# A macaron block on one core: the first stage's routing ahead of its shared expert, two bias adds on GpSimd, attention in two parts

## The chip, the cores and the metric

The kernel runs on 1 core of one Trainium2 chip, as one program. The metric is the device time of one execution in microseconds (us). Engines are named as the profile names them: PE (TensorE: matmul, and PEld its weight loads), DVE (VectorE), ACT (ScalarE), POOL (GpSimd), SP (SyncE, which here only issues DMA transfers). Each engine executes its own instruction stream in order and waits on semaphores for the others.

## The reference

The input is 8 batches of 1024 tokens of 256 values, fp32. A half-weighted feed-forward layer, linear attention and a second half-weighted feed-forward layer (same weights) follow each other, each on the layer norm of its input and added to it:

```python
x = x + 0.5 * ffn(layernorm(x))
x = x + attn(layernorm(x))
x = x + 0.5 * ffn(layernorm(x))

def ffn(xf):                      # xf: 8192 tokens x 256
    weights, idx = gate(xf)       # softmax over 16 experts; best 2 of the 4 groups, then the top 2
    combine = (one_hot(idx, 16) * weights[..., None]).sum(1)
    h1 = einsum('td,edi->tei', xf, We1) + be1      # 16 experts, inner size 128
    h3 = einsum('td,edi->tei', xf, We3) + be3
    yo = einsum('tei,eid->ted', silu(h1) * h3, We2) + be2
    y = einsum('te,ted->td', combine, yo)
    z = silu(xf @ ws1 + bs1) * (xf @ ws3 + bs3) @ ws2 + bs2   # shared expert, inner size 256
    return y + z

def attn(x):                      # per batch, 16 heads of 16 channels
    q, k, v = split(x @ w_qkv.T)
    q, k = relu(q), relu(k)
    z = 1 / (sum_n(k) . q + eps)
    context = v k^T               # per head, 16 x 16
    return (context q * z) @ w_proj.T + b_proj
```

Only the two chosen experts of a token are computed: tokens are scattered to rows of their experts in DRAM, processed there in blocks of rows, and the results are gathered.

## The kernel before, in words

All of it is one program with an automatic scheduler: the source issues work as Python generators that are advanced in turn (`run`), and the scheduler then orders each engine's instructions by their dependencies and that order of issue; only the expert blocks and the tail are in an order written out by hand. It has five stages, divided by barriers in the program's order.

- **Stage A** (rounds r = 0 to 8). Round r computes the layer norm of batch r (`normed`: L253 to L270) and its transposes (L283, L286), the routing of batch r-1 (`route`, L314) and the shared expert of batch r-2 (`shared_units`, L831). Of `route`, the gate's product pgT (L323), softmax, choice of groups and experts on DVE (L339 to L406), the rank of each token in its expert by a matmul (prk, L416), the row numbers rowi (L449) and weights cw (L433), and then on POOL the 16 scatters of rows (L467), four of them behind one iota (L456) and one tensor_scalar (L461). Of `shared_units`, per half batch: the bias bs2 (halved in `hb2`) is added to x on DVE (`add_bias`, L806), then p_s (L796), the activation and product hs_s (L800, L801), py_s (L815), and the addition to x (L819). Batch 7's routing is only begun here, and batch 7's shared expert is `late`: it is done from the end of blocks 0 on, with its bias behind the hidden layer. Finished x of batches 0 to 4 are stored to `xk` in DRAM.
- **Blocks 0** (`blocks`, L612). The scattered rows come back as xg, expert by expert: transposes pxg (L678), q (L699), hb (L705, L706), qy (L725), yo (L731), a scatter to ys (L736). The bias rows b2 (2.1 MB, loaded by SP at L236) lie in a pool of SBUF that is shared, by turns, with four of the six slots of xnT (`half`, L218; `shared_room["turn"]`); two slots are kept outside the pool. SP issues b2's loads first, then the first xg. All experts' weights are in `wall`, loaded once.
- **Stage C** (rounds r = 0 to 9). Round r advances together: `finish(r-2)`, which is the second norm and routing and then stores x to `xk` (L1056) and xnT to `xt`; `attention(r-1)`; `begin(r)`, which adds the experts' results y to x (`combine`, L856) and computes attention's norm and transposes; and the shared expert of batches 5 to 7. The x of batches 3 to 7 is loaded from `xk` (L110) at the start of the round before, into the slot of a batch that has been stored.
- In `attention` (L862), the bias of the projection is added to x first (L867, DVE, 128x2048). Then per tile of 128 tokens pk = k and q (L877), relu on ACT (L881, L882), and the products pgs (L885) summed over the batch; these are copied to gk (L892). From gk come dg (L896), pks (the sum of k, L901), pgt (L909); then on DVE q times the sum (L920), its sum per head (L923), its reciprocal, and q scaled (L929); pcx, pm (L946), the transposes of q (pt_q, L283), pp (L954), and the addition to x (L958). q lies in slots of `xn`, qk in slots of `k`, qT in slots of xnT.
- **Blocks 1** and the **tail**: the same blocks for the second layer, then the shared expert of batches 0 to 4, the gathered y and the output. They are not edited.

## Time and profile before

| what | value |
|---|---|
| time, median of 4 runs | 1370.07 us (1368.14 to 1380.86) |
| the profiled execution's own time | 1364.59 us |
| its span in the profile | 1362.9 us, mean granted PE clock 0.948 |
| stage A, to PE's last work | 0 to 235.7 us: PE busy 195.3, DVE 160.3, POOL 124.4 |
| PE waits for the first block's rows | 235.7 to 248.7 us |
| blocks 0 | 248.7 to 515 us: PE busy 226.6 |
| stage C | 515 to 990.4 us: PE busy 422.0, DVE 313.3, POOL 134.3 |
| blocks 1 | 990.4 to 1251 us: PE busy 228.6 |
| tail | 1251 to 1363 us: PE busy 104.0 |

The profile is of one execution. Busy times of different engines overlap, so they don't add up to the length of a stage. The ranks prk (L416) are computed once per batch and are used as marks: in stage A they start at 36.1, 66.5, 96.3, 124.4, 156.8, 187.9 and 216.9 us. In stage C the mark is attention's pks and pgt (L901, L909), at 571.5, 610.4, 658.6, 710.0, 763.7, 815.3, 859.9 and 927.0 us. Waits are given as the waiting engine, tile and line, then the one that it waited for. Matmuls of fp32 take two hardware instructions, so the counts are twice those in the code.

### The profile page before, as it was taken

The numbers are of one execution on the slowest core, as the hardware profiler recorded it, in microseconds if no ns is written. First come the engines' busy times: TensorE is split into PE (matmuls) and PEld (weight loads), VectorE is DVE, ScalarE is ACT, GpSimd is POOL, SyncE is SP. The second block draws the span as 40 slices with busy tenths as digits, with TensorE's granted clock in tenths as the row PEclk, the third lists the DMA queues.
The fourth block names the chain that finished last, engine by engine and source line by source line (L and its number), as shares of the span: only waits on it lengthen the run. The fifth ranks groups of instructions, "written<-read, shape, count | busy, mean of one in ns | idle before, by whom it ended". The sixth has DMA issues, their size and how long they took to land. (4 is left out here: it accounts for less than half of the span.)

```text
span 1362.9 us, 20671 instructions
## 1 busy us (share of the span) xinstructions
PE 1176.6 (86%) x5728; PEld 844.0 (62%) x5728; DVE 884.2 (65%) x2878; ACT 539.7 (40%) x1120; POOL 585.9 (43%) x719
## 2 busy tenths in 40 slices
PE   7899778687789987999878879899998888998997
PEld 3465444576678874566546546555576677886554
DVE  6786547575456667767748648627686545665687
ACT  6566422221225542554453544543422223553110
POOL 1566556376655651002252252350536665565010
PEclk9999889798999998999889889999998899999999
DMA  9334323466565534632452430110435565552996
GB/s 358 140 126 168 122 90 119 141 189 184 184 188 173 171 121 148 212 123 97 138 203 87 132 126 29 37 64 1 157 114 170 179 198 170 150 173 90 334 373 247
DMA packets 96102, 212.20 MB, mean 156 GB/s; under 512 B 17382, under 2 KB 45291, under 8 KB 92273
## 3 DMA queue, kind: packets, MB, share of 16 engines
q1 hardware_dynamic: 68288, 134.77, 31.4%
q0 software_dynamic: 27696, 76.07, 15.0%
q8 instruction: 49, 0.80, 0.3%
q14 instruction: 69, 0.56, 0.1%
HBM read 110.75 MB, written 102.64 MB: 157 GB/s over the span
## 5 line engine op out<-in xcount | busy, mean ns | idle before, releaser
L736 POOL DMA_INDIRECT ys_d<-yo,at x276 | 278.5, 1009 | 226.5 <-DVE rest L731 161.7
L699 PE MATMUL q<-xgT,wc 128*128 128x128 f32 (+1 forms) x1568 | 283.5, 330 | 60.3 <-ACT xgT L683 41.9
L467 POOL DMA_INDIRECT xs_d<-xn_f,rowi x256 | 265.2, 1036 | 110.7 <-issue 60.8
L699 PEld LDWEIGHTS q<-xgT,wc 128*128 128x128 f32 x1568 | 231.5, 196 | 88.7 <-ACT xgT L683 52.6
L683 ACT COPY xgT<-pxg 128x512 f32<-128x512 f32 x138 | 81.3, 590 | 283.3 <-PE pxg L678 132.0
L796 PE MATMUL p_s<-xnT_f,ws_sb 128*128 128x512 f32 x352 | 168.2, 618 | 0.9 <-ACT hs_s L800 0.8
L706 DVE SCALAR_TENSOR_TENSOR hb<-q,wc,hb 128x128 f32<-128x128 f32 (+1 forms) x196 | 73.5, 400 | 132.6 <-PE q L699 42.6
L725 PE MATMUL qy<-wall,hb 128*128 x552 | 146.2, 388 | 6.8 <-DVE rest L731 6.6
L731 DVE CUSTOM_DVE_ANT_0 yo<-qy,b2c,at 128x256 f32<-128x256 f32 x276 | 122.8, 482 | 43.3 <-PE qy L725 7.3
L815 PE MATMUL py_s<-ws_sb,hs_s 128*128 128x256 f32 x512 | 128.6, 393 | 17.0 <-DVE hs_s L801 9.1
L815 PEld LDWEIGHTS py_s<-ws_sb,hs_s 128*128 128x128 f32 x512 | 96.4, 195 | 52.4 <-issue 16.8
L877 PE MATMUL pk<-wqk_sb,xnT_a 128*128 128x512 f32 x256 | 125.4, 607 | 0.5 <-ACT q L882 0.3
L461 POOL TENSOR_SCALAR xn_f<-cw 128x4 f32<-128x4 f32 x64 | 17.1, 274 | 248.0 <-DVE cw L433 245.1
L725 PEld LDWEIGHTS qy<-wall,hb 128*128 128x128 f32 x552 | 103.0, 196 | 21.5 <-issue 7.4
L800 ACT ACTIVATE hs_s<-p_s,bc 128x512 f32<-128x512 f32 x64 | 43.8, 687 | 182.0 <-PE p_s L796 124.4
L796 PEld LDWEIGHTS p_s<-xnT_f,ws_sb 128*128 128x128 f32 x352 | 68.1, 199 | 66.9 <-issue 62.2
L705 ACT ACTIVATE hb<-q,wc 128x128 f32<-128x128 f32 (+1 forms) x196 | 75.4, 421 | 69.9 <-PE q L699 37.2
L678 PE MATMUL pxg<-ident,xg 128*128 128x128 f32 x552 | 84.3, 277 | 12.9 <-DMA xg<-xs_d 12.9
L678 PEld LDWEIGHTS pxg<-ident,xg 128*128 128x128 f32 x552 | 69.8, 143 | 27.5 <-DMA xg<-xs_d 13.3
L801 DVE SCALAR_TENSOR_TENSOR hs_s<-p_s,bc,hs_s 128x512 f32<-128x512 f32 x64 | 47.7, 746 | 58.1 <-PE p_s L796 42.1
L885 PE MATMUL pgs<-xn_a,k 128*128 128x257 f32 x256 | 72.5, 400 | 8.2 <-issue 3.7
L796 PE MATMUL p_s<-xnTr,ws_sb 128*128 128x512 f32 x160 | 70.4, 593 | 0.3 <-PEq L786 0.3
(302 smaller groups left out, 1735.7 us busy)
## 6 DMA issues: line engine op xcount, KB each, us to landing
xg<-xs_d SPq DMA_DIRECT2D x80, 264.0 KB
y<-ys_d SPq DMA_DIRECT2D x64, 256.0 KB
y<-ys_d SPq DMA_DIRECT2D x32, 512.0 KB
xg<-xs_d SPq DMA_DIRECT2D x116, 132.0 KB
xk<-x SPq DMA_DIRECT2D x8, 1024.0 KB
x<-xk SPq DMA_DIRECT2D x8, 1024.0 KB
wall<-in_wexp_dram SPq DMA_DIRECT2D x4, 1540.0 KB
x<-in_x_dram SPq DMA_DIRECT2D x6, 1024.0 KB
```

The costliest lines, as they stand in the source:

```text
L467: nc.gpsimd.indirect_dma_start(out=v[:, :], out_offset=bass.IndirectOffsetOnAxis(ap=rowi[:, j, k : k + 1], axis=0), in_=xn[:, t, :], in_of ...
L678: nc.tensor.transpose(pt[:, c, s * P : (s + 1) * P], xg[i][:, s, c * P : (c + 1) * P], ident[:],)
L683: nc.scalar.copy(xgT[i][:], pt[:])
L699: nc.tensor.matmul(pt_[:, cs], w[:, s, o + c * P : o + (c + 1) * P], t[:, c, cs], start=(c == 0), stop=(c == NC - 1),)
L705: nc.scalar.activation(h[:, cs], p1[:, cs], AF.Silu, bias=w[:, s, W2 - 2 : W2 - 1])
L706: nc.vector.scalar_tensor_tensor(h[:, cs], p3[:, cs], w[:, s, W2 - 1 : W2], h[:, cs], ALU.add, ALU.mult)
L725: nc.tensor.matmul(py[:, s : s + 1, :], h[:, s * P : (s + 1) * P], w2s[s % len(w2s)], start=True, stop=True,)
L731: nc.vector.tensor_tensor_reduce(out=yo[:, s, :], in0=py[:, s, :], in1=b2c[s % len(w2s)][:, 0, :], scale=a[:, s, 1:2], scalar=0.0, op0=ALU ...
L736: nc.gpsimd.indirect_dma_start(out=ys_views[i * NR + s][:, :], out_offset=bass.IndirectOffsetOnAxis(ap=a[:, s, 0:1].bitcast(I32), axis=0), ...
L796: nc.tensor.matmul(pt[:], w[:, c, s * P : (s + 1) * P], xnT[:, c, :], start=(c == 0), stop=(c == NC - 1),)
L815: nc.tensor.matmul(py[:, t - t0, :], hs[s][:, t * P : (t + 1) * P], ws2_sb[:, s, :], start=(s == 0), stop=(s == NS - 1),)
L877: nc.tensor.matmul(pk.rearrange("p k d -> p (k d)"), tile_of(axnT, c, j), wqk_sb[:, c, :], start=(c == 0), stop=(c == NC - 1),)
```

## The change

Three edits.

First, in stage A `routed(b)` is the norm and the routing of the same batch, in the same round, and is advanced five steps for every two of the shared expert of batch r-2 (`weave`). Second, `hb2` is no longer added in stage A but in `begin(b)` of stage C, ahead of the y adds, and the projection's bias in `attention_q`; both are done by GpSimd, two adds of 128x1024 each per batch. The shared expert of the second layer keeps its bias add on DVE. Third, attention is split: `attention_k(b)` (k, q, pgs, gk) runs at the end of round b+1, `attention_q(b)` (the rest) in round b+2, beside `begin(b+2)` and `finish(b-1)`; stage C has 11 rounds instead of 10. q, qk and qT lie in space lent from `wall`, the part of experts 5 to 15, which is loaded again at the end of round 9. pcx moves from a PSUM buffer of tag p3 to one of tag y. The store of x to `xk` is issued at the start of `finish`, the loads of x at the end of a round.

```diff
@@ -141,10 +141,22 @@
     wv_sb = wp.tile([P, NC, D], F32, name="wv_sb")
     wproj_sb = wp.tile([P, NC, D], F32, name="wproj_sb")
 
+    HALF = TPB * D
+    E_KEPT = E - -(-8 * HALF // WROW)
+    def lent(i, name):
+        o = E_KEPT * WROW + i * HALF
+        return wall.rearrange("p e w -> p (e w)")[:, o : o + HALF]
+    def load_experts(lo):
+        for g in range(4):
+            es = slice(lo + g * (E - lo) // 4, lo + (g + 1) * (E - lo) // 4)
+            nc.sync.dma_start(out=wall[:, es, :], in_=wexp[:, es, :])
     def load_late_weights():
-        for g in range(4):
-            es = slice(g * E // 4, (g + 1) * E // 4)
-            nc.sync.dma_start(out=wall[:, es, :], in_=wexp[:, es, :])
+        load_experts(0)
         nc.sync.dma_start(out=wqk_sb[:], in_=w_qkT.rearrange("(c p) f -> p c f", p=P))
         nc.sync.dma_start(out=wv_sb[:], in_=w_v.rearrange("(c p) f -> p c f", p=P))
         nc.sync.dma_start(out=wproj_sb[:], in_=w_projT.rearrange("(c p) f -> p c f", p=P))
@@ -274,9 +286,9 @@
                 if t == HT - 1:
                     yield
 
-    def transposed(xns, name, res):
+    def transposed(xns, name, res, places=None):
         for nb, xn in enumerate(xns):
-            xnT = half("xnT", [P, NC, TB], f"xnT_{name}_{nb}")
+            xnT = places[nb] if places else half("xnT", [P, NC, TB], f"xnT_{name}_{nb}")
             for c in range(NC):
                 pt = ps_m.tile([P, TPB, P], F32, tag="m", name=f"pt_{name}_{nb}_{c}")
                 for t in range(TPB):
@@ -802,9 +814,9 @@
             h[:], p3[:], bc[:, NS + s : NS + s + 1], h[:], ALU.add, ALU.mult
         )
 
-    def add_bias(xh):
-        nc.vector.tensor_tensor(
-            xh, xh, hb2[:].unsqueeze(1).to_broadcast([P, HT, D]), ALU.add
+    def add_bias(xh, bias=hb2, engine=nc.vector):
+        engine.tensor_tensor(
+            xh, xh, bias[:].unsqueeze(1).to_broadcast([P, HT, D]), ALU.add
         )
 
     def outputs(xh, hs, name):
@@ -828,14 +840,14 @@
     def half_of(xt, nb):
         return xt[:, nb * HT : (nb + 1) * HT, :]
 
-    def shared_units(xt, xnT, name, late_bias=False):
+    def shared_units(xt, xnT, name, bias=True, late=False):
         for nb in range(NB):
             xh = half_of(xt, nb)
-            if not late_bias:
+            if bias:
                 add_bias(xh)
             hs = []
             for s in range(NS):
-                if late_bias and nb == 0:
+                if late and nb == 0:
                     hs.append(spare(f"hs_{name}_{nb}_{s}"))
                 else:
                     hs.append(
@@ -843,8 +855,6 @@
                     )
                 hidden(xnT[nb], s, hs[s], f"{name}_{nb}")
                 yield
-            if late_bias:
-                add_bias(xh)
             yield from outputs(xh, hs, f"{name}_{nb}")
 
     def combine(which, b, xt):
@@ -859,19 +869,19 @@
             yield
 
 
-    def attention(b, xt, axn, axnT):
-        kh, qh = [], []
+    def attention_k(b, axn, axnT):
+        kh = []
+        qh = [
+            lent(b % 2 * NB + nb, "q").rearrange("p (j d) -> p j d", d=D) for nb in range(NB)
+        ]
         pgs = [
             ps_h.tile([P, D + 1], F32, tag="p3", name=f"pgs_{b}_{c}") for c in range(NC)
         ]
-        nc.vector.tensor_tensor(
-            xt[:], xt[:], bpj[:].unsqueeze(1).to_broadcast([P, NT, D]), ALU.add
-        )
         for j in range(NT):
             nb, t = divmod(j, HT)
             if t == 0:
                 kh.append(half("k", [P, HT, D], f"k_{b}_{nb}"))
-                qh.append(half("xn", [P, HT, D], f"q_{b}_{nb}"))
             pk = ps_h.tile([P, 2, D], F32, tag="p1", name=f"pk_{b}_{j}")
             for c in range(NC):
                 nc.tensor.matmul(
@@ -890,6 +900,14 @@
         gk = big.tile([P, NC, D + 1], F32, tag="wc", name=f"gk_{b}", bufs=3)
         for c in range(NC):
             nc.scalar.copy(gk[:, c, :], pgs[c][:])
+        products[b] = (gk, qh)
+        yield
+    def attention_q(b, xt):
+        gk, qh = products.pop(b)
+        for nb in range(NB):
+            add_bias(half_of(xt, nb), bpj, nc.gpsimd)
 
         dg = mid.tile([P, NC, P], F32, tag="hb", name=f"dg_{b}", bufs=3)
         for c in range(NC):
@@ -916,9 +934,9 @@
         qT = []
         for nb in range(NB):
             den = rp.tile([P, HT, H], F32, tag="den", name=f"den_{b}_{nb}", bufs=1)
-            qk = half("k", [P, HT, D], f"qk_{b}_{nb}")
+            qk = lent(2 * NB + nb, "qk").rearrange("p (j d) -> p j d", d=D)
             nc.vector.tensor_tensor(
-                qk[:], qh[nb][:], ksb[:].unsqueeze(1).to_broadcast([P, HT, D]), ALU.mult
+                qk, qh[nb], ksb[:].unsqueeze(1).to_broadcast([P, HT, D]), ALU.mult
             )
             nc.vector.tensor_reduce(
                 den[:], qk.rearrange("p j (h d) -> p j h d", d=HD), axis=AX.X, op=ALU.add
@@ -933,7 +951,7 @@
 
         cm = mid.tile([P, NC, P], F32, tag="hb", name=f"cm_{b}", bufs=3)
         for c2 in range(NC):
-            pcx = ps_h.tile([P, P], F32, tag="p3", name=f"pcx_{b}_{c2}")
+            pcx = ps_y.tile([P, P], F32, tag="y", name=f"pcx_{b}_{c2}")
             for c in range(NC):
                 nc.tensor.matmul(
                     pcx[:], wv_sb[:, c, c2 * P : (c2 + 1) * P],
@@ -946,7 +964,10 @@
             nc.tensor.matmul(pm[:], cm[:, c2, :], wproj_sb[:, c2, :], start=True, stop=True)
             nc.scalar.copy(mm[:, c2, :], pm[:])
         yield
-        yield from transposed(qh, f"q{b}", qT)
+        places = [
+            lent(3 * NB + nb, "qT").rearrange("p (c n) -> p c n", c=NC) for nb in range(NB)
+        ]
+        yield from transposed(qh, f"q{b}", qT, places)
         for j in range(0, NT, 2):
             pp = ps_y.tile([P, 2, D], F32, tag="y", name=f"pp_{b}_{j}")
             for t in range(2):
@@ -972,6 +993,19 @@
                 if next(g, StopIteration) is StopIteration:
                     live.remove(g)
 
+    def weave(many, few):
+        run(many and groups(many, 5), few and groups(few, 2))
+    def groups(gen, n):
+        live = True
+        while live:
+            for _ in range(n):
+                live = live and next(gen, StopIteration) is not StopIteration
+            if live:
+                yield
     xns, xnTs = {}, {}
 
     def normed(which, b):
@@ -984,27 +1018,35 @@
 
     LATE = 3
     base = new_base(0)
+    begun = {}
+    def routed(b):
+        yield from normed(0, b)
+        if b == B - 1:
+            begun["maps"] = first_map(base, 0)
+        routing = route(base, 0, b, xns.pop(b), xnTs[b], b == B - 1)
+        if b == B - 1:
+            begun["routing"] = routing
+            routing = part(routing, 2)
+        yield from routing
     for r in range(B + 1):
         if r == 1:
             load_late_weights()
         if 2 <= r + 1 < B:
             xs[r + 1] = load_x(r + 1, x_v[r + 1])
         s = r - 2
-        routing = None
-        if r >= 1:
-            routing = route(base, 0, r - 1, xns.pop(r - 1), xnTs[r - 1], r == B)
-        if r == B:
-            maps, done, fill = first_map(base, 0)
-            steps = behind(routing, base, 0, maps, done, fill)
-        if r == B - 1:
-            run(routing)
-        run(
-            normed(0, r) if r < B else None,
-            routing if r < B else part(routing, 2),
-            shared_units(xs[s], xnTs.pop(s), f"s0_{s}") if s >= 0 else None,
+        weave(
+            routed(r) if r < B else None,
+            shared_units(xs[s], xnTs.pop(s), f"s0_{s}", False) if s >= 0 else None,
         )
         if 0 <= s < B - LATE:
             nc.sync.dma_start(out=xk_d[s][:], in_=xs.pop(s)[:])
+    maps, done, fill = begun["maps"]
+    steps = behind(begun["routing"], base, 0, maps, done, fill)
     tc.no_sync_barrier()
 
     def park(b, j):
@@ -1033,7 +1075,7 @@
         moves += [partial(fetch, b, j) for j in range(NT)]
 
     s = B - 1
-    late = shared_units(xs[s], xnTs.pop(s), f"s0_{s}", True)
+    late = shared_units(xs[s], xnTs.pop(s), f"s0_{s}", False, True)
     blocks(maps, 0, steps, by_block(moves), partial(steps_of, late, NS))
     for b in range(B - LATE, B - 1):
         xs.pop(b)
@@ -1042,18 +1084,23 @@
 
     room("rows1")
     base = new_base(1)
-    axns, last = {}, []
+    axns, products, last = {}, {}, []
 
     def begin(b):
+        for nb in range(NB):
+            add_bias(half_of(xs[b], nb), hb2, nc.gpsimd)
         yield from combine(0, b, xs[b])
         axns[b] = ([], [])
         yield from layernorm(xs[b], f"a{b}", axns[b][0], D + 1)
         yield from transposed(axns[b][0], f"a{b}", axns[b][1])
 
     def finish(b):
+        if b < B - LATE:
+            nc.sync.dma_start(out=xk_d[b][:], in_=xs[b][:])
         yield from normed(1, b)
         if b < B - LATE:
-            nc.sync.dma_start(out=xk_d[b][:], in_=xs.pop(b)[:])
+            xs.pop(b)
             for nb in range(NB):
                 nc.sync.dma_start(out=xt_d[b][nb], in_=xnTs[b][nb][:])
         if b == B - 1:
@@ -1064,21 +1111,25 @@
             routing = part(routing, 2)
         yield from routing
 
-    for r in range(B + 2):
-        if LATE <= r + 1 < B - 1:
-            xs[r + 1] = load_x(r + 1, xk_d[r + 1])
-        s = r - 3
+    for r in range(B + 3):
+        s = r - 4
         run(
             late if r == 0 else None,
-            finish(r - 2) if r >= 2 else None,
-            attention(r - 1, xs[r - 1], *axns.pop(r - 1)) if 1 <= r <= B else None,
+            finish(r - 3) if r >= 3 else None,
+            attention_q(r - 2, xs[r - 2]) if 2 <= r <= B + 1 else None,
             begin(r) if r < B else None,
             shared_units(xs[s], xnTs.pop(s), f"s1_{s}") if s >= B - LATE else None,
         )
+        if 1 <= r <= B:
+            run(attention_k(r - 1, *axns.pop(r - 1)))
         if r == 0:
             nc.sync.dma_start(out=xk_d[B - 1][:], in_=xs.pop(B - 1)[:])
-        if r == B - 2:
-            xs[B - 1] = load_x(B - 1, xk_d[B - 1])
+        if LATE <= r + 1 < B:
+            xs[r + 1] = load_x(r + 1, xk_d[r + 1])
+        if r == B + 1:
+            load_experts(E_KEPT)
     s = B - 1
     run(shared_units(xs[s], xnTs.pop(s), f"s1_{s}"))
     tc.no_sync_barrier()
```

## What I predict

> **What bounds the kernel now.** I read the page's head first, then the busy time by windows cut at the rank matmuls (prk, L416, one per batch), then the waits, then the groups. The profiled execution is 1364.59 us (span 1362.9); the median of the runs shown is 1370.07, 5.5 us more. I work against the first and add 5.5 at the end.
>
> Page, engines: busy us (share of span).
>
> ```profile
> span 1362.9 us, 20671 instructions
> PE 1176.6 (86%) x5728; PEld 844.0 (62%) x5728; DVE 884.2 (65%) x2878; ACT 539.7 (40%) x1120; POOL 585.9 (43%) x719
> ```
>
> TensorE (PE) is the busiest engine, but 86% is a mean. By stage: 0 to 235.7 us the first norm, routing and shared expert (stage A); 248.7 to 515 the expert blocks (blocks 0); to 990.4 combine, attention, second norm and routing (stage C); to 1251 blocks 1; then the tail. Only A and C are edited. Windows, one line per round, of A and then of C (columns: length, then busy us and count of PE, PEld, DVE, ACT, POOL; granted PE clock; DMA share; GB/s):
>
> ```profile
> 36.00:66.00 30.00, 24.56 (x117) 14.69 (x118) 21.86 (x87) 18.39 (x27) 17.57 (x24) 0.99 0.41 144
> 66.00:96.00 30.00, 28.45 (x123) 17.30 (x123) 26.84 (x83) 17.09 (x29) 20.95 (x24) 0.90 0.39 138
> 96.00:124.00 28.00, 25.93 (x121) 15.00 (x120) 21.79 (x75) 15.69 (x24) 18.57 (x27) 0.99 0.44 158
> 236.00:249.00 13.00, 0.34 (x2) 0.34 (x3) 1.76 (x6) 0.00 (x0) 5.94 (x10) 0.63 0.61 222
> ```
>
> ```profile
> 610.00:658.00 48.00, 42.11 (x218) 27.73 (x210) 31.91 (x101) 22.41 (x50) 17.60 (x26) 0.94 0.47 158
> 658.00:710.00 52.00, 42.10 (x206) 27.48 (x203) 34.56 (x104) 25.76 (x58) 17.89 (x27) 0.93 0.45 151
> 710.00:763.00 53.00, 45.01 (x197) 30.44 (x199) 34.80 (x103) 25.14 (x55) 17.29 (x25) 0.85 0.40 133
> 860.00:927.00 67.00, 62.32 (x265) 40.08 (x264) 34.20 (x87) 28.84 (x59) 21.90 (x31) 0.97 0.11 41
> ```
>
> A round of A lasts 30 us. Its matmuls at full clock (p_s 128x512 at 0.43 us, py_s 128x256 at 0.215, transposes 0.11) add up to 24.8. A round of C lasts about 50 for 38.2 of such work. No engine is full: a round is one long dependency through DVE, ACT and PE in turn, and PE, busy part of the time at a clock of 0.85 to 0.94, pays twice. The last two rounds of C differ: shared-expert work fills them (62 of 67 busy), so a shorter chain is worth nothing there.
>
> The waits say which steps end late (us in total, times, longest):
>
> ```profile
> POOL xn_f L461 <- DVE cw L433: 245.1, 14, 40.5
> DVE dg L896 <- ACT gk L892: 33.0, 8, 10.1
> DVE x L856 <- DMA x<-xk: 23.3, 4, 11.1
> PE pxg L678 <- DMA xg<-xs_d: 12.9, 1, 12.9
> ```
>
> The scatter engine (POOL) waits for the routing, attention's second half waits in DVE for its first (4.1 us a batch), and PE stands still for 12.9 us before blocks 0, since the last scatters end after its work. Prices come from the groups:
>
> ```profile
> L467 POOL DMA_INDIRECT xs_d<-xn_f,rowi x256 | 265.2, 1036 | 110.7 <-issue 60.8 <-ACT xnT_f L286 13.0 <-ACT xnT_q L286 12.2
> L806 DVE TENSOR_TENSOR x<-x,hb 128x1024 f32<-128x1024 f32 x28 | 33.9, 1214 | 9.9 <-ACT xn_f L270 8.3 <-issue 1.3 <-DVEq L786 0.3
> L456 POOL IOTA xn_f<- 128x32 f32 x64 | 12.1, 196 | 78.6 <-PE pgs L885 75.9 <-PE pgT L323 1.2 <-DMA xs_d<-xn_f,rowi 0.7
> L867 DVE TENSOR_TENSOR x<-x,bpj 128x2048 f32<-128x2048 f32 x5 | 11.4, 2280 | 0.0
> ```
>
> **Part 1, stage A.** Routing of batch r now shares a round with its own norm and is issued five steps to two of shared(r-2). In the changed program's order of PE work, about 20 us lie between two ranks (24.8 before) and 37 us behind the last free rank, prk_6 (18.8 before): nothing is saved on PE, the shared expert slides behind the routing. On DVE, windows 36 to 124 hold 70.5 busy us in 88, 24.0 per 30. Two bias adds of 1.21 leave each round (-2.4), and a sixth of one batch's shared steps (four L801 at 0.75 and four L819 at 0.69, 5.7 us) slides behind prk_6 (-0.95): 20.6. I keep the present ratio of round to DVE work, 30/24 = 1.25, because the chain stays the same: 25.8 us a round. The ranks run from 36.1 to 36.1 + 6 x 25.8 = 190.9; with 37 behind, PE ends at 228. The 16 scatters of batch 6 (16 x 1.34 with their gap of 0.3, 21 us after the rank) are then done, so the 12.9 us wait goes. Next late is SyncE's queue (SP): the 2.1 MB load of b2 (L236) waits for shared(6)'s last p_s in both versions, and the first xg load is queued behind it. I take 6 us for this instead of 12.9: 234 against 248.7, **-15**. Ends: rounds of 22.5 (near PE's 20) give -35, rounds still of 30 give +10.
>
> **Part 2, stage C.** The bias of attention's projection leaves DVE: 2.28 us a batch. With attention_k finished in the round before, dg need not wait: 4.1 us a batch. The chain through DVE's in-order queue shortens by 6.4, in the six rounds that PE does not fill: -38. The loads of x (L110) now go out at a round's end, after a store moved to its start, so SP no longer holds them for the norm's reading (SPq L1056 waited 61.2 us in four); I count the 23.3 us of DVE's waiting for them neither as gained nor as lost, because the loads also start later.
>
> POOL gets 32 adds of 128x1024, for 16 such adds of stage A's DVE work (14 of them in the rounds) and 8 of twice the size. The trace has no such add on POOL. Below, the same shape on DVE: 1.21. Above, the 128x32 iota row with all its time put down to elements: 0.196 x 32 = 6.3. I take 2.4, nearer the DVE row, which is the same operation and shape. The 16 of attention_q are read only a round later (L958) and hide behind POOL's wait for the routing (245.1 us in 14). The 16 of begin do not all: for b = 5 to 7 they stand behind eight scatters of another batch (8 x 1.34 = 10.7 and 1.0 of small instructions), so x's first half is ready 11.7 + 2.4 = 14.1 us after that batch's row numbers (rowi). DVE's queue reaches the y add (L856) some 8.5 us after rowi: two dg at 0.29, two q products at 1.22 and a sum at 1.21 (L920, L923), 1.0 of small ones, and 3 for PE's pks and its copy. It stops there for 5.6, and behind it stand the second q product (L929) and, through that, PE's pt_q. DVE later makes some up; I take 4 a round: 3 x 4 = **+12**. Together -26; the ends are -38 (no stall) and the rival below.
>
> [...]
>
> **Part 3, what the split's buffers bring.** q, qk and qT lie in the space of experts 5 to 15, which are loaded again (4.3 MB) in the last rounds: at the 222 GB/s of the window 236 to 249 that is 19 us, beside some 45 us of shared-expert work, so nothing; without that cover it would be 19. qT no longer takes xnT slots, so their turn shifts: b2 of blocks 1 now needs the slot that shared(7) reads last. SP's waits before:
>
> ```profile
> SPq L236 <- PE pp L954: 141.7, 1, 141.7
> SPq L236 <- PE p_s L796: 62.2, 1, 62.2
> ```
>
> The first is b2 of blocks 1, let go 35 us before stage C's end. Now it goes 3.4 us before that end, with the first xg behind it: 2.1 MB at 222 GB/s is 9.4, one xg about 1, so PE stands still some 7 us, and restarts at half speed, which cost 2.3 us at 248.7 (pxg and q of the first block 5.3 against 2.9): **+9** (ends 0 and 16).
>
> Blocks 0, blocks 1 and the tail keep their instructions: 0. Sum: -15 - 26 + 9 = -32, 1332.6; with the 5.5, **1338**.
>
> **Rivals.** (1) *The waits go entirely*: rounds of A at 22.5, no POOL stall: -35 - 38 + 9 = -64, 1306. For: PE has only 20 us between ranks. Against: DVE alone needs 20.6, in a serial chain. (2) *Stage A's rounds keep 30 us*, since the routing's serial chain sets them, now within one round after its own norm: the 37 us behind prk_6 then lengthen the stage, +10 - 26 + 9 = -7, 1363. For: nothing is full today. Against: seven rounds interleave and the order gives routing precedence. (3) *GpSimd's adds sit on the chain*, the slower case: place, the two adds of begin ahead of each batch's y adds. At 6.3 us an add, three rounds lose 8 more (+24) and the other five up to 8 (+40): 1402. Each us above 2.4 costs 2 x 8 = 16, so from about 4.4 us on the gain is gone. For: POOL runs in order and its scatters come first. Against: at 2.4 most of it lies in POOL's idle time, 30 of 50 us.
>
> **Chances.** Forecast 0.47, (1) 0.11, (2) 0.22, (3) 0.20. A measurement of this kernel tells about 1% from no change (1356 to 1384). Faster: 0.45 + 0.11 + 0.04; within: 0.02 + 0.16 + 0.03; slower: 0.02 + 0.17. The range, 1304 to 1388, leaves out half of (1) and half of (3), 0.15; the forecast's own is 1318 to 1357.
>
> **What would show it.** Right: ranks of A some 26 us apart; DMA wait before blocks 0 near 6; rounds of C at 44 to 48; no dg wait; SPq L236 waiting for p_s twice, and a gap of 7 before blocks 1. Wrong: POOL adds above 4 us, y adds waiting for POOL, or DVE instructions such as L856 longer than 0.69 while POOL adds.

## The result

The changed kernel takes 1375.82 us (median of 52 runs, 1367.12 to 1394.24), the kernel before 1369.88 (78 runs) on the same chip: a ratio of 1.0048, 95% interval 1.0034 to 1.0062. I had predicted 1338, so the forecast gain of 32 us is not there. The outcome is the "within 1%" to which I gave 0.21.

The runs of this study fell on chips of two kinds. On some the kernel before takes 1370 to 1390 us, the trace of before among them; on others it takes 1241 to 1243. I call these the 1370 kind and the 1242 kind. Every ratio below is against the kernel before on the same chip.

Page of the changed kernel, first profiled execution (1385.52 us, 10 above its median); columns as before:

```profile
span 1383.6 us, 20674 instructions
PE 1173.8 (85%) x5728; PEld 851.9 (62%) x5728; DVE 891.2 (64%) x2854; ACT 538.1 (39%) x1118; POOL 661.1 (48%) x751
```

DVE lost 24 instructions and still is 7 us busier; POOL is 75 us busier. The waits of the same execution that answer to those shown of before, and SP's for b2:

```profile
POOL xn_f L473 <- DVE cw L445: 115.0, 10, 28.6
DVE x L866 <- POOL x L818: 22.2, 4, 7.5
DVE dg L914 <- ACT gk L902: 21.0, 7, 8.5
PE pxg L690 <- DMA xg<-xs_d: 11.7, 2, 5.9
...
SPq L248 <- PE p_s L808: 88.1, 2, 44.2
```

Two waits are as predicted: 12.9 us before blocks 0 became 5.9, and there is a second such gap before blocks 1, with SP waiting for p_s twice. The wait for gk shrank by a third only, and y adds (L866) now wait for POOL.

Stage by stage I compare two other executions, nearer to the medians: of the kernel before (run before_again) and of the changed kernel (after_again). The windows are cut at the first block, the end of blocks 0, the first block of blocks 1 and its end; the first and the third row (stages A and C) are shown, the kernel before first.

```profile
0.00:245.80 245.80, 193.25 (x869) 113.17 (x869) 161.58 (x532) 114.47 (x181) 130.91 (x193) 0.93 0.44 163
...
508.80:990.20 481.40, 429.84 (x1863) 278.85 (x1862) 314.03 (x858) 219.82 (x469) 135.73 (x193) 0.93 0.32 110
```

The changed kernel:

```profile
0.00:257.70 257.70, 197.52 (x870) 116.20 (x870) 148.09 (x519) 113.54 (x180) 126.08 (x193) 0.92 0.42 157
...
525.60:991.90 466.30, 406.72 (x1863) 267.26 (x1861) 333.01 (x849) 218.02 (x468) 216.93 (x223) 0.94 0.35 121
```

Stage A is 11.9 us longer although DVE has 13.5 us less to do, stage C 15.1 shorter although DVE has 19 more. Blocks 0 take 4.9 more, blocks 1 2.9, the tail 0.6. Sum +5.2; the spans differ by 5.3. Single executions of this kind vary: the first block comes at 248.7 and 245.8 us in the two traces of the kernel before, and at 267.2 and 257.7 in those of the changed kernel, so stage A is 9 to 21 us longer; blocks 0, which the change doesn't touch, take 267.4 and 263.0 us before, 269.4 and 267.9 after. The same pair of kernels on chips of the other kind (runs before_third and after_third):

| stage, us | before, 1370 kind | changed | before, 1242 kind | changed |
|---|---|---|---|---|
| A, to the first block | 245.8 | 257.7 | 215.3 | 205.6 |
| blocks 0 | 263.0 | 267.9 | 228.4 | 228.7 |
| C, to blocks 1 | 481.4 | 466.3 | 459.7 | 464.1 |
| blocks 1 | 265.6 | 268.6 | 226.5 | 230.6 |
| tail | 111.9 | 112.5 | 111.5 | 111.6 |

The total is nearly unchanged on both kinds, for opposite reasons: on the first stage A loses and stage C gains, on the second it is the other way round.

### The profile page after: what moved, and what is told of

Read it like the earlier page. It is cut to its first block, busy times and chain, and to the rows that moved or that the text cites. A ratio compares the mean times of both kernels' runs of the same rounds, so it can differ in the third digit from the quotient of the medians.

```text
span 1383.6 us, 20674 instructions
## 1 busy us (share of the span) xinstructions
PE 1173.8 (85%) x5728; PEld 851.9 (62%) x5728; DVE 891.2 (64%) x2854; ACT 538.1 (39%) x1118; POOL 661.1 (48%) x751
## 5 line engine op out<-in xcount | busy, mean ns | idle before, releaser
L711 PE MATMUL q<-xgT,wc 128*128 128x128 f32 (+1 forms) x1568 | 288.9, 334 | 63.9 <-ACT xgT L695 38.7
L479 POOL DMA_INDIRECT xs_d<-xn_f,rowi x256 | 264.8, 1034 | 111.9 <-issue 63.5
L711 PEld LDWEIGHTS q<-xgT,wc 128*128 128x128 f32 x1568 | 235.6, 199 | 91.1 <-ACT xgT L695 46.9
L827 PE MATMUL py_s<-ws_sb,hs_s 128*128 128x256 f32 x512 | 133.1, 407 | 26.8 <-DVE hs_s L813 18.9
L827 PEld LDWEIGHTS py_s<-ws_sb,hs_s 128*128 128x128 f32 x512 | 101.4, 204 | 64.2 <-DVE hs_s L813 28.1
L717 ACT ACTIVATE hb<-q,wc 128x128 f32<-128x128 f32 (+1 forms) x196 | 75.0, 418 | 85.6 <-PE q L711 42.7
L473 POOL TENSOR_SCALAR xn_f<-cw 128x4 f32<-128x4 f32 x64 | 16.1, 257 | 143.8 <-DVE cw L445 115.0
L831 DVE SCALAR_TENSOR_TENSOR x<-py_s,x 128x512 f32<-128x512 f32 x56 | 38.1, 688 | 60.9 <-PE py_s L827 23.9
```

The costliest lines, as they stand in the source:

```text
L479: nc.gpsimd.indirect_dma_start(out=v[:, :], out_offset=bass.IndirectOffsetOnAxis(ap=rowi[:, j, k : k + 1], axis=0), in_=xn[:, t, :], in_of ...
L711: nc.tensor.matmul(pt_[:, cs], w[:, s, o + c * P : o + (c + 1) * P], t[:, c, cs], start=(c == 0), stop=(c == NC - 1),)
L717: nc.scalar.activation(h[:, cs], p1[:, cs], AF.Silu, bias=w[:, s, W2 - 2 : W2 - 1])
L827: nc.tensor.matmul(py[:, t - t0, :], hs[s][:, t * P : (t + 1) * P], ws2_sb[:, s, :], start=(s == 0), stop=(s == NS - 1),)
```

## What holds stage C: GpSimd's adds hold DVE off

The y adds show it. Before, none of them waited for GpSimd and one took 0.69 us in the mean (group line: count, busy us, mean ns, idle time before):

```profile
L856 DVE TENSOR_TENSOR x<-x,y 128x512 f32<-128x512 f32 x40 | 26.9, 686 | 26.6 <-DMA x<-xk 23.3 <-DMA y<-ys_d 3.1
```

Source view of the changed kernel's first profiled execution (count: ns minimum/median/maximum, first and last start):

```profile
L866 DVE TENSOR_TENSOR x<-x,y x40: 621/680/3020, 596.8 to 816.5; 128x512 f32<-128x512 f32 x40
L818 POOL TENSOR_TENSOR x<-x,hb x10: 2341/2350/2807, 582.9 to 801.2; 128x1024 f32<-128x1024 f32 x10
L979 DVE TENSOR_TENSOR x<-pp,x x20: 676/692/692, 762.9 to 952.3; 128x512 f32<-128x512 f32 x20
L265 DVE BATCH_NORM_STATS2 st_a<-x x40: 375/396/426, 631.7 to 826.8; 128x6 f32<-128x256 f32 x40
```

A GpSimd add takes 2.35 to 2.8 us, near the 2.4 I took. But a y add of 0.68 us takes up to 3.02, its own time and a whole GpSimd add. The additions of pp, one of whose inputs is in PSUM, and bn_stats, with one input, never take longer, although 7 of the first and 21 of the second overlap a GpSimd add. Set beside the GpSimd adds by their times, 20 of the 64 y adds overlap one and take 2.2 us on average: 31 us of DVE in all, and 2.4 more in L947. It goes both ways: the ten of the 32 GpSimd adds that take over 2.55 us all began while a DVE instruction with two SBUF inputs ran.

The cost could be DVE's waiting for x, DVE being held off while GpSimd adds, or the adds' place in GpSimd's queue, so I took them apart.

**Both biases back on DVE** (run bias_dve), everything else as changed:

```diff
-            add_bias(half_of(xs[b], nb), hb2, nc.gpsimd)
+            add_bias(half_of(xs[b], nb), hb2)
...
-            add_bias(half_of(xt, nb), bpj, nc.gpsimd)
+            add_bias(half_of(xt, nb), bpj)
```

> The changed kernel with both biases added by DVE at their new places (32 adds of 1.21 us). If GpSimd's adds sit on the chain, stage C gets shorter and the time falls below 1370 us. If they are hidden and DVE's queue is what the rounds wait for, 39 us more work on DVE in stage C lengthens its eight rounds by some 1 to 2.4 us each: 1384 to 1395 us.

1189.29 us against 1242.04, ratio 0.9586 (0.9545 to 0.9627). The changed kernel itself, on the same chip, was 0.9973 (0.9954 to 0.9992; run after_third below): 48 us of its time by the ratios, 52 by the medians, are GpSimd's adds. Stage C takes 411.5 us there instead of 464.1, although DVE does 39 us of adds itself. Source view of bias_dve:

```profile
L866 DVE TENSOR_TENSOR x<-x,y x40: 619/678/693, 487.1 to 664.9; 128x512 f32<-128x512 f32 x40
```

**Only bs2 back on DVE** (run hb_dve, the first line of that diff):

> The changed kernel with bs2's adds (those just ahead of the y adds) back on DVE at their new place, the projection's bias still on GpSimd. If the cost lies in y adds that are held while a GpSimd add of the same batch runs (21 y adds of 2.2 us instead of 0.68 in the trace) and in the wait for the first of them, nearly all of the 45 us go: 1190 to 1200 us. If every GpSimd add costs about the same wherever it stands, half: about 1215.

0.9894 (0.9823 to 0.9965) on a chip of 1370 us, where the changed kernel is 1.0027: 19 us of the time go. Stage C takes 440.2 us instead of 466.3, so 26 go there; in this execution stage A and blocks 0, which the edit doesn't touch, are 7 and 6 us longer. The 16 adds of bpj that stay still hold DVE for some 25 us, y adds of another batch (up to 2.93 us) and bias adds among them. A GpSimd add need not touch the same batch to cost something. The expected figures were for the other kind of chip, so "nearly all" and "half" aren't told apart by this run alone (19 of 48 to 52 would be under half, but the second figure is of the other kind); the next two are cleaner.

**Extra adds that nobody waits for** (lock_add), and **iotas in their place** (lock_iota). The base, dve_gate, has both biases on DVE and b2's gap closed (below). GpSimd works besides on the space of two experts' weights, which are loaded again afterwards, twice per batch beside each of the two biases (lock_iota has an iota of the same 128x1024 in the place of each add):

```diff
+    free = wall.rearrange("p e w -> p (e w)")[:, 3 * WROW : 3 * WROW + HALF]
+    scratch = free.rearrange("p (j d) -> p j d", d=D)
...
             add_bias(half_of(xs[b], nb), hb2)
+            add_bias(scratch, hb2, nc.gpsimd)
...
             add_bias(half_of(xt, nb), bpj)
+            add_bias(scratch, bpj, nc.gpsimd)
...
-            load_experts(E_KEPT)
+            load_experts(3)
```

> As the first of these, and GpSimd does 32 more adds of 128x1024 in stage C, on a space that nobody else reads or writes then (two experts' weights, loaded again afterwards; the adds are extra work that the result does not use). No instruction waits for them but GpSimd's own later ones. If GpSimd and DVE hold each other off, DVE's instructions with two SBUF inputs (y adds L866, q products L938 and L947, bias adds) that meet an add take up to 3 us instead of 0.7 to 1.2, those with one input or PSUM keep their times, and the total rises by 10 to 40 us. If the cost of the changed kernel's adds was only their place in the queue, DVE's durations stay and the total rises by less than 5 us.

> As the one above with 32 iotas of 128x1024 in the place of the adds: GpSimd is occupied too and writes the same space, but reads no SBUF. If it is GpSimd's reading that holds DVE off, DVE's durations stay as they are without, and the total rises by less than 5 us. If any long GpSimd instruction holds DVE off, it costs in proportion to its time like the adds.

On one chip, where the kernel before takes 1390.23: base 1353.09 (0.9725, 0.9668 to 0.9782), with adds 1398.41 (1.0044, 1.0012 to 1.0076), with iotas 1351.36 (0.9699, 0.9641 to 0.9758). So 32 adds that no instruction of DVE waits for cost 45 us, and 32 iotas nothing that the intervals show. In stage C of the profiled executions the same instructions keep DVE busy for 332.9 us in the base, 376.8 with the adds and 333.1 with the iotas; the stage lasts 434.6, 472.4 and 432.4 us. Source views, lock_add:

```profile
L866 DVE TENSOR_TENSOR xf<-xf,y x24: 654/2257/2484, 559.3 to 634.9; 128x512 f32<-128x512 f32 x24
...
L818 POOL TENSOR_TENSOR wall<-wall,hb x16: 1995/2328/2861, 552.7 to 620.2; 128x1024 f32<-128x1024 f32 x16
L265 DVE BATCH_NORM_STATS2 st_a<-xf x24: 386/393/417, 576.1 to 636.7; 128x6 f32<-128x256 f32 x24
```

and lock_iota:

```profile
L866 DVE TENSOR_TENSOR xf<-xf,y x24: 636/681/694, 552.0 to 586.5; 128x512 f32<-128x512 f32 x24
L1100 POOL IOTA wall<- x16: 989/999/1001, 547.6 to 576.7; 128x1024 f32 x16
```

In lock_add the y adds of the first three batches, nearly all inside the stretch of GpSimd's adds, take 2.26 us in the middle instead of 0.68; bn_stats in the same stretch takes 0.39, with the iotas 0.40. An iota occupies GpSimd for 1.0 us, an add there for 2.33; 20 y adds overlapped an iota and none got longer (0.69 at most). So in these runs it is neither GpSimd's queue nor its being busy for 1.0 us at a time. The adds read SBUF and the iotas don't; that the reading is what counts is my inference from this pair. Beside the adds DVE's instructions with two SBUF inputs got longer by up to a whole GpSimd add (3.02 us, against 0.68 and 2.35, in the changed kernel), while those shown above with a PSUM input (0.69 at most) or with one input (0.43 at most) kept their times. In all DVE is held for 33 us in the changed kernel and for 44 in lock_add.

## The split and its eleventh round

**Attention whole again**, in ten rounds, the rest as changed (run unsplit):

```diff
-            finish(r - 3) if r >= 3 else None,
-            attention_q(r - 2, xs[r - 2]) if 2 <= r <= B + 1 else None,
+            finish(r - 2) if r >= 2 else None,
+            attention(r - 1, xs[r - 1], *axns.pop(r - 1)) if 1 <= r <= B else None,
...
-        if 1 <= r <= B:
-            run(attention_k(r - 1, *axns.pop(r - 1)))
```

> The changed kernel with attention whole again, in ten rounds; the lent space, the biases on GpSimd and the places of the x store and load stay. If the split's shorter rounds are paid back by the eleventh round, the first pks comes some 20 us earlier, the rounds are again near 50 us, and the total is within 8 us of the changed kernel, 1368 to 1384. If the split is worth its shorter rounds (7 us each over seven), the time is 1400 or more.

1283.20 us, 1.0328 (1.0284 to 1.0372), against 0.9973 with the split: the split is worth 42 us here, and my expectation that it pays itself back falls. Its rounds (pks to pks) are 45.8, 40.8, 56.8, 57.0, 57.5, 48.6 and 68.1 us; with the split 41.3, 40.6, 46.6, 47.8, 47.9, 41.4 and 37.2 (after_third). The eleventh round costs what I had overlooked, but less: the first pks comes at 76.4 us after blocks 0 instead of 68.1, and the last pks lies 84.9 us ahead of blocks 1 instead of 64.6. That is 29 of the 72 us that seven rounds bring. The price is at the end above all: with both biases on DVE and the split in place (bias_dve) the first pks comes 58.9 us after blocks 0, nearly as early as before the change (56.6, before_third), while the last still lies 84.8 us ahead of blocks 1. With attention whole, GpSimd's adds of bpj stand in the middle of a batch's own chain and hold more of it: y adds took up to 5.1 us, and even a 128x64 tensor_scalar with one tensor input, 0.185 us in the middle, took up to 4.7, while two GpSimd adds ran:

```profile
L938 DVE TENSOR_SCALAR den<-den x16: 176/185/4707, 509.0 to 887.0; 128x64 f32<-128x64 f32 x16
```

So in that run two SBUF inputs aren't the only sign of an instruction held beside GpSimd's adds. What the split is worth with the biases on DVE wasn't measured by itself.

**b2's gap** (run gate): one line after the opening of stage C's room,

```diff
     room("rows1")
+    shared_room["turn"] = NXT - NXT_KEPT
```

> The changed kernel with the turn of the xnT slots begun four places later in stage C, so that shared(7)'s inputs lie in the two slots outside the pool that b2 takes. If the gap of 6 us before blocks 1 comes from b2's wait for shared(7)'s last p_s, the gap goes, SP no longer waits for p_s there, and the time is 6 to 8 us lower, about 1369. If something else ends just as late (the expert weights' reload, the rows' own load), the gap stays and the time too, about 1376.

1233.81 us, 0.9935 (0.9906 to 0.9965), 8 us below the changed kernel on that chip; the PE gap before blocks 1 is gone and SP waits for p_s 24 us less. Blocks 1 are 3.4 us shorter too (227.2 instead of 230.6): in the 4 us from their start PE's granted clock is 1.00, where it was 0.50 after the gap (after_third). This step was predicted at +9 and measures 5.3 of gap and 4 of restart (blocks 1 took 226.5 us in before_third).

**Both together** (dve_gate) were expected thus:

> The changed kernel with both biases on DVE at their new places and the turn of the xnT slots begun four places later in stage C. The two edits gave 0.959 and 0.9935 of the kernel before one by one; if they act in different places they add to 0.95 to 0.955 of it. If the shorter stage C only moves the wait to another transfer, 0.96.

0.9725, above both expected figures, but on a chip of 1390 us; the two single figures were of the other kind, and the estimate does not carry over. What carries over is that with both biases on DVE and the gap closed the changed kernel is faster than the kernel before there too.

## Stage A

**The order alone** (a_only: the kernel before with the changed rounds and weave, bs2 left in place):

```diff
...
-        run(
-            normed(0, r) if r < B else None,
-            routing if r < B else part(routing, 2),
+        weave(
+            routed(r) if r < B else None,
             shared_units(xs[s], xnTs.pop(s), f"s0_{s}") if s >= 0 else None,
...
```

> The kernel before with stage A's new order alone: routing of a batch in the round of its norm, five steps to two of the shared expert, biases left on DVE in their old places. If the new order shortens or lengthens nothing by itself (ranks as far apart as before, 8 us more shared work behind the last rank against a shorter wait for the first rows), 1238 to 1248 us. If, as I had predicted, it brings 15 us, 1227.

1375.46, 1.0021 (0.9987 to 1.0056): nothing. The first block starts at 247.3 us (before: 245.8), and only 18 us lie between the last free rank and PE's last work of the stage (22 in before_again, 19 in the first trace). So while bs2 is in place the new order slides no shared work behind the routing; its expected time was for the other kind of chip.

**The old order without bs2** (a_before: the changed kernel with stage A's old rounds):

```diff
...
-        weave(
-            routed(r) if r < B else None,
+        run(
+            normed(0, r) if r < B else None,
+            routing if r < B else part(routing, 2),
             shared_units(xs[s], xnTs.pop(s), f"s0_{s}", False) if s >= 0 else None,
...
```

> The changed kernel with stage A's rounds put back (norm of batch r, routing of r-1, shared expert of r-2 advanced one step each); bs2 stays out of stage A, stage C stays changed. If the new order itself lengthens stage A (ranks still about 30 us apart, and 37 us of shared work behind the last free rank instead of 19), the first block starts again at about 246 us instead of 267 and the time is about 1358 us, 18 below the changed kernel. If the longer stage A of the profiled execution is an accident of that execution, or is due to the moved bias, the time stays at 1372 or more.

0.9961 (0.9942 to 0.998), the first block at 203.6 us. This chip is of the 1242 kind, where the changed kernel's first block comes at 205.6: the two orders are 2 us apart, not 18. PE's last work of the stage ends 28.5 us after the last free rank here, 18.9 in before_third and 37.7 in after_third: bs2's leaving slides some 10 us of shared work there, and the new order, once bs2 is gone, 9 more. I therefore looked at the rounds themselves, on both kinds. The changed kernel, rounds from rank 1 on, first after_again (1370 kind), then after_third (1242 kind):

```profile
59.70:94.70 35.00, 25.29 (x107) 16.02 (x108) 19.83 (x71) 20.19 (x32) 17.54 (x26) 0.79 0.20 74
94.70:124.80 30.10, 24.03 (x110) 14.94 (x110) 17.76 (x66) 13.97 (x21) 17.34 (x24) 0.89 0.38 138
```

```profile
54.30:79.10 24.80, 22.89 (x108) 14.99 (x109) 19.90 (x71) 21.27 (x36) 19.25 (x28) 0.87 0.29 106
79.10:100.60 21.50, 20.94 (x109) 13.24 (x109) 17.33 (x66) 12.84 (x21) 15.79 (x23) 1.00 0.51 186
```

The kernel before, first on the 1370 kind (before_again), then on the 1242 kind (before_third):

```profile
96.30:124.70 28.40, 25.61 (x121) 14.85 (x120) 21.52 (x74) 15.63 (x24) 18.89 (x26) 1.00 0.43 156
86.50:112.80 26.30, 25.48 (x120) 14.81 (x119) 21.24 (x74) 15.55 (x24) 20.59 (x27) 1.00 0.49 173
```

In the 1242 kind's two rows at full clock PE is 97% busy, and over all six rounds 90 to 100% in both kernels: a round *is* the PE work between two ranks, here 26.3 us before and 21.5 after. On the other kind the same 110 matmuls take 24.0 us at a clock of 0.89, and 6 us stand idle. The idle time is of a particular sort. Waits of after_again:

```profile
ACT xgT L695 <- remote: 49.1, 9, 10.2
...
ACT gT L340 <- remote: 19.5, 4, 7.3
...
PE pg L344 <- issue: 13.6, 4, 7.1
```

gT copies the result of pgT from PE. In after_third the copy starts 0.07 to 0.4 us after pgT's last matmul; in after_again it starts up to 7.8 us after it, with PE and ACT nearly idle, and PE's pg waits behind it. "Remote" and "issue" say that the profile has no work to name for it (the traces of the 1370 kind hold about half as many semaphore records, 11857 against 21220 for these two, so a name can be missing); the late starts themselves are read from the times, and after_third has none for gT and pg. From rank 1 to rank 6 gT's late starts sum to 17 us, of the 47 by which these five rounds are longer than in after_third; the rest isn't taken apart. The blocks lengthen by the same kind of gap: counted from the end of their matmuls, or of ACT's instruction before, the copies xgT start 87 us late in all in after_again, 10 in after_third, and the two block stages are 77 us longer. The tail, which has no scatters, doesn't lengthen (112.5 and 111.6). I don't know what delays these handovers on those chips, nor whether it is the chip or something that ran beside the kernel.

**The bare rounds**, the kernel before without the shared expert of batches 0 to 6 (those results are left out):

```diff
-            shared_units(xs[s], xnTs.pop(s), f"s0_{s}") if s >= 0 else None,
+            None,
```

> The kernel before without the shared expert of batches 0 to 6 in stage A (these results are left out; the later stages run as they are). What is left of a round is norm, transposes, routing and scatters: 21 us of scatters on GpSimd, some 16 us of DVE. If a round's length comes from the shared expert's steps standing between those of the routing in the engines' queues, ranks are 21 to 23 us apart, as the scatters allow. If it is the routing's own chain, 28 to 30 as before.

> The kernel before without the shared expert of batches 0 to 6 in stage A, once more. On a chip of 1370 to 1390 us: if a round's length there is the routing's own chain, with late handovers from engine to engine, ranks stay 27 us apart or more although PE has hardly any work; if it is the work of PE between the ranks, 20 to 23 us as on the other chip, where they were 22.4 apart. On a chip of 1242 us nothing new: 22 us.

Both landed on chips of the 1242 kind: ranks 22.4 and 22.2 us apart in the mean (16 to 30 singly), with PE busy for 7 of 24 us and POOL for 18. Routing alone takes about as long as GpSimd needs for its scatters (an estimated 21 us, 16 x 1.34 from the trace of before), and the norm waits for scatters to have read its rows (ACT xn_f for DMA, 27 us in the three rounds from 74 us on); the changed kernel's 21.7 us are already there. What the bare rounds take on a chip of the other kind wasn't measured, so that the routing's chain is what keeps ranks 30 us apart there, whatever PE's work, stays an inference from the gaps above.

## The whole on each kind of chip, and a better version

The changed kernel twice more, and the kernel before for its traces:

> The changed kernel itself, unaltered, beside the same runs of the kernel before as the other kernels of this chip, where the kernel before takes 1242 us instead of 1370. By the variants already measured there (undoing the order 0.996, the b2 gap 0.9935 of before) it should be at 0.996 to 1.002 of the kernel before. If the first result depends on its chip, it comes out elsewhere: 0.98 or 1.02.

> The kernel before, for its profile on this chip. Expected: 1242 us; ranks of stage A about 22 us apart instead of 30, and no waits of 2 to 10 us for which the profile shows no work, if those belong to the first chip. If they belong to the kernel, ranks 30 us apart here too.

> The changed kernel once more. On a chip where the kernel before takes 1242 us: stage A 9 us shorter (first block at 206 us against 215), stage C some 4 us longer, 0.996 to 0.999 of the kernel before. On a chip where it takes 1370 to 1390: first block 10 to 18 us later, 1.001 to 1.008.

> The kernel before, for its profile beside the three others of this chip. Expected: 1370 to 1390 us and ranks of stage A 30 us apart, or 1242 and 22, by the chip.

after_again: 1375.26, 1.0027 (0.9986 to 1.0068), on the 1370 kind. after_third: 1241.41 against 1243.03, 0.9973 (0.9954 to 0.9992). before_again took 1369.44, with ranks 29.7 us apart, before_third 1243.16, with 23.7. after_again and before_again were expected on a chip of the 1242 kind and fell on the other, so 0.996 to 1.002 isn't tested by the first. The stage A of after_third was expected 9 us shorter and its stage C 4 longer; they came 9.7 shorter and 4.4 longer.

**The version that beats both** keeps the split and bs2's new place, puts both biases on DVE, stage A's old rounds back and b2's slot right (best: the edits of a_before, bias_dve and gate together):

> As the one above, and stage A's rounds as in the kernel before, but still without bs2. If the sliding of shared work behind the last rank is what lengthens stage A, the first block starts some 3 us earlier (or some 10 where rounds are 30 us): 0.94 to 0.952 of the kernel before. If the order of stage A is worth nothing, the same as the one above.

> The split of attention with bs2 moved into stage C, both biases on DVE, stage A's rounds as before and the later turn of the xnT slots, on this chip. It was 0.964 of the kernel before elsewhere; expected 0.94 to 0.97. Its stage A, without bs2's adds, is as long as that of the kernel before if those adds cost nothing there, 2 to 17 us shorter if they do, and longer if it is their absence that lets shared work slide behind the last rank.

0.964 (0.9578 to 0.9701) on the 1390 us chip, 1340.34 us, above the expected 0.952 there but 13 us below dve_gate; 0.9488 (0.9463 to 0.9512) on one of 1241 us, 1178.51 us. Beside it on the latter, with bs2 left in stage A (c_alone):

```diff
-            shared_units(xs[s], xnTs.pop(s), f"s0_{s}", False) if s >= 0 else None,
+            shared_units(xs[s], xnTs.pop(s), f"s0_{s}") if s >= 0 else None,
...
-    late = shared_units(xs[s], xnTs.pop(s), f"s0_{s}", False, True)
+    late = shared_units(xs[s], xnTs.pop(s), f"s0_{s}", True, True)
...
-        for nb in range(NB):
-            add_bias(half_of(xs[b], nb), hb2)
```

> As the one above, but bs2 is added in stage A as in the kernel before, so that its stage A is that of the kernel before and stage C has 16 DVE adds less. If the whole gain lies in stage C, the first block starts with the kernel before's, and the total is at or below the one above: 0.94 to 0.965. If moving bs2 is worth its 17 us of DVE in stage A, it is above it: 0.97 or more.

1188.44, 0.9564 (0.9537 to 0.9591). Against the kernel before (before_third), its stage A is the same (215.7 and 215.3 us to the first block) and its stage C 53.3 us shorter (406.4 instead of 459.7): that is the split with all that belongs to it (lent space, pcx's buffer, the places of the loads and stores, b2's slot). Moving bs2 (best_again) brings stage A to 202.6 us, 13 shorter, and costs 2.8 in stage C, on DVE. So not all of the gain lies in stage C.

## Why the prediction was wrong

- **Stage A, -15 predicted, +11.9 measured** on the chip of the trace. The failing step is "I keep the present ratio of round to DVE work, 30/24 = 1.25". Rounds went from 29.7 to 30.4 us, not to 25.8. DVE's work did fall (161.6 to 148.1 us in the stage) and PE's work between ranks too, and neither was what ended the rounds there. The rest of the step held or came early: first rank at 31.7 (36.1 predicted), 37.5 us behind the last free rank (37), 6.1 us of gap (6): 31.7 + 6 x 30.4 + 37.5 + 6.1 = 257.7. With rounds of 25.8 the same sum gives 230. This is rival 2, priced at +10. On chips without the late handovers the step gives -9.7, for another reason than mine: PE's work between ranks. What keeps the rounds at 30 us on the other kind stays open; late handovers account for a part.
- **The signs of that were in the first trace.** Waits on "remote" of up to 13 us stood among its rows (7.8 in stage A), and PE was busy for only 25 to 28 us of 28 to 32 at a clock of 0.87 to 0.99. I read the round as "one long dependency through DVE, ACT and PE in turn" and left unasked why that dependency was so slow.
- **Stage C with its gap, -17 predicted, -15.1 measured there**: the sum is right by luck. The rounds became shorter by more than I said: seven rounds from 362.6 to 304.8 us, -57.8, where I had -38 + 12. I had no term for the stage's two ends: first pks 74.3 us after blocks 0 instead of 58.2, last pks 87.2 ahead of blocks 1 instead of 60.6, together +42.7. The 26.6 at the end are the eleventh round with b2's gap (5.3); the 16.1 at the start are GpSimd's adds for the most part, since with both biases on DVE the first pks comes at 58.9 instead of 76.4 on the other kind. On the other kind of chip the same step measured +4.4.
- **GpSimd's price** per add was right (2.35 to 2.8 us against 2.4), what it does was not. "3 x 4 = +12" counted the wait of the y add for its bias only: 22.2 us in four waits. It left out the y adds and products that run while an add runs: 33 us of DVE. The 16 adds of attention_q, taken as hidden, alone hold DVE for 25 (hb_dve). The sum had no term for DVE being held while an add runs, since no row of the trace of before shows it; two signs that the prediction named against itself (y adds waiting for POOL, L856 longer than 0.69) both came, the second with 3.02 us (L866 of the changed kernel). End to end the adds cost 45 to 52 us, more than the whole forecast gain of 32. Rival 3 named the place and set the point from which GpSimd decides at 4.4 us an add. That point was wrong, because the price per add there was the queue's alone; at 2.4 us the adds already cost at least as much as the split brings beside them (42 us, unsplit).
- **dg's wait**, counted as gone (4.1 us a batch), went from 33.4 us to 20.2, and on the 1242 kind grew from 11.2 to 18.6. In six of the eight batches DVE comes to dg right behind the row numbers (L461) of another batch, and gk ends only 1.4 to 3.0 us later: attention_k is issued at the very end of the round before, so that little work lies between it and dg.
- **The reload of experts 5 to 15** costs nothing, as said: no wait for it is among the traces' waits. b2's gap and restart: +9 predicted, 9.4 measured on the 1242 kind (5.3 of gap, 4.1 of longer blocks 1); the half speed of the restart is a granted clock of 0.50 from 249 to 252 us in the trace of before.

## What to carry to other kernels

Before moving elementwise work from DVE to GpSimd, list DVE's instructions that have two SBUF inputs in the same stretch, and watch the others too (L938 in unsplit): here the 20 y adds that overlapped a GpSimd add took 2.2 us on average instead of 0.68, and one long instruction took the engines behind it along (PE's pt_q waited 23 us in five times for L947, 3.66 us at the longest). A pipeline deepened by one round has a price of its own, here 20 us, without b2's gap, at the end, to be set against what each round saves. And before extrapolating the length of a round, ask what ends it: if no engine is full and waits have no named cause, a ratio to one engine's work says nothing about what less of that work will bring.

## What was not expected of the hardware

- Chips differ: the same kernel took 1241 to 1243 us on two of them and 1369 to 1390 on at least two others. In the changed kernel's two traces the median durations of each kind of instruction agree within 3%, and handovers between engines come up to 8 us late on the latter kind. An edit's sign in one stage depended on it (stage A: -9.7 and +11.9). The cause is open.
- 32 GpSimd adds of 128x1024 that nothing on DVE waits for cost 45 us; 32 iotas of the same shape, 1.0 us each, cost nothing.
- Less PE work in a round doesn't always mean a shorter round: on the 1370 kind 110 matmuls took 24.0 us, at a granted clock of 0.89, where they take 20.9 at 1.00, and 6 us more stood idle. Whether the idle time lowered the clock isn't shown: the row with 9.7 us idle has 0.79, but one with 1.9 has 0.87.
